# A deformable-convolution, causal-attention and mixture-of-experts kernel: new lengths for the maxima's way and a new written order, the causal mask of the second score pass moved to GpSimd, late weights laid over other room, scatters by pairs of images

## The chip, the cores and the metric

The kernel runs on one core of one Trainium2 chip. The metric is the device time of one execution in microseconds (us). It is the median over the runs that were made. The engines are named as in the profile: PE (TensorE matmul), PEld (its weight load), DVE (VectorE), ACT (ScalarE), POOL (GpSimd) and SP (SyncE, which here only issues DMAs).

## The reference

The input `x` holds 8 images of 56 x 56 positions with 128 channels, so 3136 tokens per image. Layer 0 is a deformable convolution with two residual blocks, layer 1 causal attention followed by a top-8 mixture of 64 experts. Cut to what matters:

```python
# layer 0
xp = x @ w_in + b_in
h = gelu(batchnorm(depthwise_conv3x3(x)))
offset, mask = h @ w_off + b_off, softmax(h @ w_msk + b_msk)      # 4 groups, 9 points
y = einsum("nghwpc,nhwgp->nhwgc", bilinear_sample(xp, offset), mask) @ w_out + b_out
x = x + gamma1 * layer_norm(y)
x = x + gamma2 * layer_norm(gelu(x @ w_fc1 + b_fc1) @ w_fc2 + b_fc2)
# layer 1
t = x.reshape(8, 3136, 128)
z = layer_norm(t)
scores = (z @ Wq) @ (z @ Wk).T / sqrt(3136)
scores = scores + -1e12 * (1.0 - tril(ones))                      # causal
t = t + softmax(scores) @ (z @ Wv)
probs = softmax(layer_norm(t) @ gate_w.T + gate_b, axis=tokens)
vals, idx = top_k(probs, 8)                                       # per image and expert
pooled = sum_k vals * t_normed[idx]
out_e = gelu([pooled, 1] @ weight1[e])  ->  [., 1] @ weight2[e]   # 64 experts, 512 hidden
t = t + scatter_add(idx, vals * out_e)
```

## The kernel before, in words

**Tiling.** An image is cut into seven chunks of 448 tokens (`CH`), and these into four groups `(b, s)` of one or two chunks, so there are 32 groups. Tiles have 128 tokens. Each stage is a generator over groups: `bring` and `prepare` load the input and project it (L496 to L543), `conv`, `plan`, `fetch`, `weigh` and `sums` do the sampled convolution (L552 to L754), `project` the two residual blocks (L819), `norm` the layer norm (L937), `scores`, `maxes`, `keyed`, `exps` and `attend` the attention, `after` its end and the gate (L1095 and after), `share` prepares the experts' shares.

In the sampled convolution `fetch` loads 1.6 MB (`g<-img`, L683) per tile over SP's queue into one of three buffers, DVE multiplies it by the taps (L707), and POOL folds it by a chain of adds (L726, 3.45 us each, then L746 to L754). For image 0 PE does the rest of the folding (L733).

**Attention.** Scores are computed twice. First with queries in the rows: `scores` (L982) writes `sc` tiles to PSUM, for diagonal tiles a second small matmul (L990, `identb` times `maskq`) adds the causal mask, and `maxes` (L1005, L1007) reduces each row to its negated maximum `neg`. Then with keys in the rows: `keyed` (L1047) writes `st`, for which the maximum of each query must be in the contraction itself. So the maxima take a way through memory: `neg` (one value per partition) is written by a DMA on ACT's queue to a row in DRAM (L1013, L1017), and a DMA on SP's queue reads that row into row 0 of `qT` (L1019). The first `st` matmul of the group needs it. Because row 0 of `zT` is 1, `st` comes out with the maximum subtracted. For the 224 pieces that cross the diagonal, a second matmul (L1055, `identb` times `maskk`) adds the mask to `st`; ACT takes the exponential into `pe` (L1068, three buffers), and `attend` multiplies it with the values (L1079). `maskk` is made at the start: GpSimd builds the mask (masks.py:30), PE transposes it (`pt_mask`, L472), ACT copies it (L474).

**What sets the order.** The steps are not ordered by a scheduler at build time. Every `yield need(engine, us, since=...)` marks one step with the engine's length in us and, in `since`, the time from which it can start. A planner, run beforehand, took these numbers and wrote the string `ORDER`, one letter for each step (`NAMES` tells which generator a letter advances). The kernel replays that string, so each engine's queue has exactly this order. The numbers in `need` don't reach the chip; they act only through the string. In `maxes` the planner is told that the read can be issued 4.0 us after the write and that the row is there 2.6 us after that.

**The end.** When all groups are projected, `give_up` (L1365) frees the convolution's room and loads the first 20 experts' weights (`weights`, L1411 and L1413: pairs of experts, 1 MB a pair, on SP's queue). After the last step of `ORDER` the work pool `wk` is closed, and a pool `fin` takes its room: 12 late experts' weights first, then the tiles `outT`, `rows`, `eh`, `hb`, `eo`, `oe`. The tail runs the experts four at a time (`hidden` L1453, `turned`, `outputs` L1482, `gathered`), between which POOL gathers the rows of the output that will be changed (`gather`). The remaining weights follow as experts are done with. At last, for each of four pairs of images, PE and DVE add the experts' outputs to the gathered rows (L1550, L1553); when all four pairs are done, one block of 32 indirect DMAs on POOL writes them back (L1558).

A second kernel in the file, taken for inputs with large offsets, is left out here.

Of the kernel before, what the change touches and what calls it, by code (L numbers as in the profile page):

```python
# [8 lines left out]
F32 = mybir.dt.float32  # L9
BF16 = mybir.dt.bfloat16  # L10
# [3 lines left out]
ALU = mybir.AluOpType  # L14
# [60 lines left out]
def need(engine, us, take=None, give=None, since=None, kind=None, when=None, lock=False):  # L75
# [27 lines left out]
    "ppppppbpbkppppbwpwwwpwpwpvkvfvvvvvvvwvpfpccpccwcpwwcbwccfcppccpcccwpcwpccpcbwcvcvcvcvcvcvccv"  # L103
    "cvvwggvvwsvwwvvvvwsvvvgfsvppcccspbccpgppbpscgcpfsscccspcpccvcfsscsvcvcvvcsmvcvcmvfvcvmcvcmvc"
    "vcvmmcvmcvmmvcvmcmvmmgmgvpbmpvgspcmpkscpvmgcfssmsmmmmmpssnpnnnnsfvncvncngpnnsnnncfspncvqqxqv"
    "qgvpgscccfxsscxxgxsvbvcssxvfccsvcgxcctscteftvstvevaevaeavacsvcvcvavocfpcospmccoompoocpcoppoc"
    "opbcbpmggcommoomosoccmococmmpomcmgcsmgmfmpmvcvcvssvcvcsoccccmfsssvcmgcmoscmgsmommfmvmvmcvsgc"
    "vmvcmskmvcmfsvmvmmgmmmcmscmcvvcvmfssvvovooopcgscpcpfssgmpcmgpppmsmmmkmpcfssnmnpgcmspmcmcfncs"
    "smncncmcnmgcscmnvcmfssnmmcmmgnsmnnvbmnvnfvnnvncgcssngcmncmnscnmvvcnfmssmmnmnmvmvnqmgcscvvkcc"
    "xqfsqxcvqmqxxqcmxqxqxcvqcxqcxbsmxqqmqxxmxqvmcmxqmvsvvvvmxfsvgpqpqcmmxgspmxmgxbmskcmpxgpmvcfs"  # L110
    "xtctectcmmcamcmsstesvcmvescvtsesvtsfcvtmtagaaeeameaevasmatatvestvenvtnsntsnnstnsfnentgvaaeae"
    "naeaevgasnvanvmntvnsnmtesctnsageseasfnatnemnacmnmsavonvmmsvnmcsmvnscvnmpcgnbmcpcvcvcoqcqxoxc"
    "qocqqcxoxcqxomxqksmsoqxfqxoqxoqxqxmoqxqxsmqxqmxcqmxsqxcqmmcqxcmxxqmqxoqxmoqxqosmoqqxoxqxqxqs"
    "xosxoqsfxomoxpmxopmgcmspmpmmosmmcxbgscvmsoscmsfocogxpttsetvtvsevaesaecvscmscvokamvfagomtcoet"
    "coamcmomtomseocseacoavostoposestssptfgetetppottsapnnannsanenpnbesnesttpntpgpabpsasfaepeeagpa"
    "etatespttvcstnvnavssavesnctfesangnteanntensvanvenvansvensvanssensfganqqqcqxcxqxqxqcxqxcxqcxq"
    "xcqxqxcqxgqccacaqqcxxcqxqcxqcxxqxqsgxcxqvcscqcsqxsvxqscxsfqxvqcxqccxqcxqsxvmqxmqxsvmxsqsvmsv"
    "qsfxqxtxtcectecsgtettsamaevaescmasvsagcfetcaetcqecqcvcqxqvxcqcxcxqcxmaxacmqcamcxcqgmmqmpobpx"
    "mxqompxopxmoppbmopomoooooxoompkmxotptemttommetmemtmptvavaevtevomvamvomevoavmavaomteetetootot"
    "ooaaemoaoaemeomemoammotmmoommotmoemooomakmaaemtmtmemtmsentnnmntnmsnannmestmtassaseamfetenmaa"  # L120
    "aetesnateanteannaesannanmgsntnstsesaesfnmtngnmnnstneaseqmqxsqxsqxssfqxqgqmamsamxxstxmmssqmsq"
    "xsfemgsxmqmstxkstemtetxsmtgssfaaeceagcsceavmmmcamsacxvsmctsvmsctvsfmgxcteteaesmavavetmcvaesv"
    "ctvsctsectsecftmctctavcaegcaeaecaevacamcapbmcpomocmmgpcmcmocmmtmcpmopccvcevvmvoktmoaootemote"
    "oteomamaematmsotaeomvtmsvemvvtsmvtstoasmaennnansmnasfnnnemeameaamanmmogcmmnmmsnmnccmsncncsnc"
    "snsvsfvovnmnvgnvnvosnvnvonvsvnksmqssqxfqcxmqxqxsqcxqxcmoqxoqmoxqoxsoqmxoqcxsmocxqvsmqsxsmxfq"
    "mcomxvcomvqqcomxqxqmcqxcmxqcxqxqmcxmcxqmcvmxcomvmxvpmcmvcbomovcmvocpvoxcooomcpkcpcxtgmttemet"
    "etpmmtmmsanaennaennnaesnnaagnottesntesoaesnasgnsfonantntteenaeatosteaoetosonoanososeonoasnos"
    "fonagnntnoqeqgxqxsoqoxqoxqoxsoqxosqxosqosxosfqxqxqxqxgmqsmmsqmqxxqssxsasfxagoqoosqoxqxmxqxqs"
    "mxqxsqsxmsqxsfmoxmogcmmsommoccsmomgsposmotbsosmfccgpsemqmqcqxxqkcmcxaxvsqmmqmsmscqmsqcxsfxcq"
    "xqxtxxtegstteaseaesqcsqcssfqxxtxtgxtetaspeaspaecpsaxcaesapsampsfnonnnnxtpeomapsogppmpstbstes"  # L130
    "bposesgftptegptavnaeavasnvnotontnosvenevtsevstnsvmsnfvtvangaeaecaecaoaocoqocooqxmqxocqmqcxxq"
    "xmcqmqcxqoxqxxqxqcoxocqxoqxoqxocomxsogqmmcqsmmocqxmsxqcoxqxqxsgcsxsfqvcvcqxoxtovtesvovtcosva"
    "evsoeavsoscavcsfcovctgoteteaecsavmccttsomtsecmscsooocfcegccpcqpcqcqxcpcxxcbapaemcqkapcxacmgc"
    "apqbmpttexpmxmaepampmtmvtevmvtmexvmvtmvttexvmavmavaeemaemmammammtmmtmememtkmttemamaemmaemsaa"
    "mstmtestetsesttsasfaeaeaeaamsanonmntsotsentmnenanensmasganftmeosnannotgntmeoetosnoanooemonos"
    "onmoomssagsnasfmnmnnmmnonmtnqqsoxqoxemxssogsososfomotqeoqxosqmxqxqxqmxkqxsomxaosmaxmsgossfto"
    "teocomgoscamoceosavooxmststsecsftcgtxetetvmasoavaecsevtevasccsvasevafcvacvmcvtmctctemgeamate"
    "tectetcvptbgcacetacaecmeamaecaapcmommocpcoptmcmocttomopomocotmomvevvcvecovcomakvmaataemotoma"
    "momomsevomvomvosnmeennonansmoansonaosomtntestmoanfeeanamaonnmnomnnsmmgcnmmnommcnscmngcmncovv"
    "cocvvsvcnovmnovkcnvonvoqscosqcxsqsmfxqxvqxqvxpoxqosqpoxqxqmxvqbxsqxmsqmxsqsxsfqxmqxpxqmmqxsm"  # L140
    "xqmpmpxsopmcsqbqscspqmxfxqcmqcpxcxmcxmxocmocmomcommocpommgoxomcpmcccoxtcvoectoctcevoteotooot"
    "oomoakmooaageoeaeamaootomtmomemstogaeotaesoaeotaetonsanteasonensanosnasnfnovmotvmovemnovovmt"
    "vsteteansaesnagsnasnsfntnteotnoaensoooatntseenstnsgtsensftnganeaneqmqxsmqxqxmsxqmqsxmsxsagms"
    "faaqeqqxsxaqxqxsaqxosxqsosqsfxoxqomxqmgsmqmmsqmsqxgsmxsxsfxgmscmoccsoqvckspsxqbpsmqocfxqxqmx"
    "qxqmqxxqxqmmpmsssxmxqmspsmxpsnfnpmnqnonqxnqpxqxqmxnoqnxmqxoqbxnmxnpoxmnonmgnmmnqmxmosoqmpmpq"
    "xxmtxoxtegttsoaetoesgaoeqsesqvsqsfoqomvgovovoocsxccxxqcxscvqcxqssxqxsqsfxcmtgmtamaetesctxakm"
    "somemaocsmaecosmcaogsmcfamomococmvqcqxocqoqmqxxqcmxqxcxqcxqxcqxtoooctcetxectvecgttsqaaevgqev"
    "axsxqeqxsmxcmssvcmscqsfqxmmxvamvxacsvacvttvetstevecasvaesmvxcsatsvfmmgtvxpmtcmscpccsaecbspsm"
    "spetkcppfgcamcaaemetcaemcmpacmmsampbmmpptsgmttstesteseasvsfaevaevavavtvmtvesvaemvatsmeststse"
    "gsftettamgasetetasaeaessaesasfatatnennaennannsnototnegteoetcnntcntcnocancnagnsenonasesnsansf"  # L150
    "eonoaonoonoomonocqmqcxqcxcqxqoxqxqxqsxoqoxoqxosmxooagsmsmosscfommoxcomcomcvscvgcsvcxvssvtcsv"
    "tsfevtexgtectctsctavaevsmvesakmcsacsfacemtgeaevaapcopmtcmmtcbemmpctpocageoceaocpaovctocvmvtm"
    "cevmcevtmvtcvtectvacvaeomaeaecomoaatomatmeoemoammaommotommoototmoemoeeoomaokatmaaomtotommeme"
    "omseanonmnnomnsntonnmeontmotoaaseaeomaanasmossosnfmnmonnmonnmosnomooonsoommonosgcnsmsnsfmnnm"
    "ccngqcvscmvxovovvmvsqkmqcqsxxqxomqxoqxosmoqsxosfqmoxqoxcqmxqxcmqsxcqmcqxcsxqoqxosxmsxqmscfmx"
    "qcmqcqxmxqxmqxqxoxmovxomvmocmmvcovcmmgmmxmcvpbmcpccgxovoctoctectgcpemetkcmtcvacvaecvtepamopp"
    "abemmpammsanmnnpmnoootsteptsnptntmnsensetsmvsfavaveaevaeatantveaetstentntsntnsngassannmfeaea"
    "smanemnamensagnntnsnestsnsgqesfqaaqxsxqxqqxxsqxqxssqxsqxsfqxqxqxtxsgteteteqsqqssxaxssfmexgcm"
    "mqmmsqcmxgcxsmcscqmsqcsxcsfmxgcccscmqcmcsqqkcvmxaxpsmabmsapqmsmqmsfxmxpmxmancqmqsxqxqxmnqxqx"
    "smpqnqsnpsnqxnqxqxsxnqcfxnmnxcqxnnxpcmxoncgmpcncmmpmconmxcbqcgmmcomxtsteomgessqpgqsxpqsxsvxq"  # L160
    "sfxqxqxqxvoaoacootocootceootceoaexmovakmvagtmtetesaeoqmmosqxomqosxoqsxosmqsofxqoxqoxvqxqxqsv"
    "qxxaxsqvosmqsoxsmxsofmgmoqmoqomqxsqmxqxxmsqxmqsxmsxsamgsfmcmmommcgstcmvotvsxtovtsvsomevssfvv"
    "egemamasaeacmootccxktsevtesvtsevstctfavxaevmtemvmamsagsaettseatesteascmscpsfmctcpmgtmpsaaeps"
    "apcbasecepsabpssafgtepettseptgptstvmavaevsavessvaesfgaemaattcevstevaveavcastctesgctesaecsasf"
    "attemeamatactnenoncenctnncntecnacoaenagamcncnomcmscogmmcscmmsvcscomstcfsvtcvtvmvcvcsvcocecsm"
    "ectkesmctsctsoancofoaeomvntevsanmnvtemagnneanseavaoasoonotntgontenasesnesmcafmnmoqqoxcqxoqoc"
    "xocpxqpcqxqxcopbocoqpcqxopcoxaoxtvgcoectcoaceovqovovtotoeteooottxavxmeavmtvemvtvmtaaemxaemaa"
    "emeamxatameommommoamoomotomotoemoeoomoakmattotmeotemmaotmemseaotnonmnnosmnnmonnsamoanooaotte"
    "moeaesmasassfemnanmnamnnmmsnsmmgcnsmmsnsnsfmnnccvncvcmnvgsvvcovcnvsvmnokvmqvsqoxqcxqmxcqxcoq"
    "xcqxvopxqbsmqmoxpqxsqmofxvqxsmqmqxmcqmcmsxqmxqxsqxxqmxqxsqmxsqsxooqfxqxmxpmxpmcmmcoocommcomm"  # L170
    "oxmocppbmocpoocoxcgotoctectctgecaeaeacacgtcmceokmatmtoetemmoemmstotmamnsnoemnootostmootosnos"
    "anmonaeoaesmnaofnatteaevtnevaovaevasnvnanvmntmntnvetsvnengeansaensoasnosnsfpnonpmnoqosqoxoqx"
# [2207 lines left out]
```

## The time and the profile before

| | |
|---|---|
| median of 3 runs | 3163.42 us (3162.01 to 3168.71) |
| profiled execution, its time | 3155.84 us |
| profiled execution, its span | 3154.0 us, mean granted PE clock 0.952 |
| PE busy in 0 to 143 us, 143 to 2921, 2921 to 3154 | 80.1 of 143, 2597.1 of 2778, 122.5 of 233 |
| DVE busy in the same stretches | 107.7, 2071.6, 84.7 |
| POOL busy in the same stretches | 73.8, 2057.1, 104.9 |
| first start of `sc` (L982), last start of `av` (L1079), weight loads | 121.1 us, 2962.2 us |
| 32 scatters (L1558), first and last issue | 3096.7, 3136.6 us, 0.98 us each |

The profile is of one execution. Its span is the time from the first to the last instruction, and the execution takes 1.8 us more. PE's busy time is high in the middle stretch, where the convolution of later images runs beside the attention of earlier ones. At the start and in the tail no engine is busy throughout. A line of the groups is: line, engine, operation, output and inputs, shapes and count, then busy time and mean of one in ns, then the idle time of the engine just before these instructions with what ended it. A line of the waits is: who waited, for what, us in total, times, the longest.

### The profile page before, as it was taken

How to read it: one execution, taken by the hardware profiler on the slowest of the kernel's cores; microseconds unless marked ns; L12 is line 12 of the kernel's file. 1: busy time of each engine (PE TensorE's matmuls, PEld its weight loads, DVE VectorE, ACT ScalarE, POOL GpSimd, SP SyncE). 2: the span in 40 equal slices, each digit the busy share in tenths (PEclk: the TensorE clock that was granted, in tenths of full speed). 3: DMA queues.
4: the chain of work that ended last, by engine and by line, in shares of the span. 5: the costliest groups of instructions: out<-in, count | busy, mean ns of one | idle time of the engine just before them, and what ended most of it. 6: DMA issues, size and time to landing. Idle time of an engine off the chain costs nothing.

```text
span 3154.0 us, 37084 instructions
## 1 busy us (share of the span) xinstructions
PE 2799.6 (89%) x11986; PEld 1655.0 (52%) x11986; DVE 2264.0 (72%) x4101; ACT 1497.9 (47%) x3489; POOL 2235.8 (71%) x2322
## 2 busy tenths in 40 slices
PE   4789899998998989998998999999998999899771
PEld 3666555555555545555555555555554555555331
DVE  6888893788768786677877788678878865467630
ACT  3444445554555435653555545644464455523310
POOL 3767784787678877688877889678977998123453
PEclk9889999999999999999999999999999999999896
DMA  6665443445353444345534445356642553030170
GB/s 175 212 217 187 149 155 76 130 147 191 118 162 116 145 138 170 95 145 166 181 128 106 167 139 190 95 139 187 184 97 87 197 163 112 23 134 12 63 282 26
DMA packets 300849, 442.45 MB, mean 140 GB/s; under 512 B 39812, under 2 KB 153996, under 8 KB 300644
## 3 DMA queue, kind: packets, MB, share of 16 engines
q1 hardware_dynamic: 184612, 382.32, 36.0%
q10 hardware_dynamic: 112768, 51.50, 7.1%
q0 software_dynamic: 3264, 6.15, 0.7%
q8 instruction: 97, 1.59, 0.2%
q14 instruction: 108, 0.88, 0.1%
HBM read 386.27 MB, written 53.81 MB: 140 GB/s over the span
## 4 chain that ended last, share of the span: by engine, by line
PE 65%; DVE 12%; DMA 11%; POOL 6%; issue 3%; ACT 2%; ACTq 0%; SPq 0%; POOLq 0%; DVEq 0%
PE sc L982 16%; PE st L1047 15%; PE av L1079 14%; DMA maxes<-neg 7%; PE ph L857 4%; PE pm L869 3%; DVE g L707 3%; DMA g<-img 2%; DVE pv L568 2%; POOL g L726 1%; DMA qT<-maxes 1%; DVE mx L1005 1%; PE py L843 1%; PE pg L1151 1%; PE pc L1108 1%
## 5 line engine op out<-in xcount | busy, mean ns | idle before, releaser
L707 DVE TENSOR_TENSOR g<-g,tp 128x3200 f32<-128x3200 f32 (+1 forms) x200 | 694.7, 3477 | 100.8 <-DMA g<-img 78.4
L1047 PE MATMUL st<-qT,zT 128*128 128x448 f32 (+8 forms) x1606 | 664.1, 537 | 114.5 <-DMA qT<-maxes 99.5
L726 POOL TENSOR_TENSOR g<-g 128x1536 f32<-128x1536 f32 (+1 forms) x200 | 690.4, 3452 | 94.1 <-DVE g L707 85.6
L1068 ACT ACTIVATE pe<-st 128x448 f32<-128x448 f32 (+8 forms) x803 | 396.5, 504 | 616.8 <-PE st L1047 327.5
L982 PE MATMUL sc<-zT,qT 128*128 128x512 f32 (+4 forms) x1594 | 620.1, 523 | 12.9 <-DVE mx L1005 12.1
L1079 PE MATMUL av<-pe,zk 128*128 128x448 f32 (+8 forms) x1606 | 617.0, 510 | 3.1 <-ACT pe L1068 2.0
L1005 DVE TENSOR_REDUCE mx<-sc 128x1 f32<-128x512 f32 (+6 forms) x797 | 442.5, 584 | 140.3 <-PE sc L982 97.5
L1047 PEld LDWEIGHTS st<-qT,zT 128*128 128x128 f32 (+1 forms) x1606 | 289.9, 199 | 358.4 <-issue 246.5
L1079 PEld LDWEIGHTS av<-pe,zk 128*128 128x128 f32 (+1 forms) x1606 | 288.3, 192 | 235.1 <-issue 182.2
L982 PEld LDWEIGHTS sc<-zT,qT 128*128 128x128 f32 x1594 | 275.9, 188 | 255.1 <-issue 122.5
L568 DVE SCALAR_TENSOR_TENSOR pv<-xg,dw,pv 128x448 f32<-128x448 f32 x448 | 307.6, 687 | 49.2 <-ACT pv L565 38.1
L746 POOL TENSOR_TENSOR g<-g 128x768 f32<-128x768 f32 (+1 forms) x175 | 317.9, 1817 | 8.9
L857 PE MATMUL ph<-xT,fc 128*128 128x512 f32 (+2 forms) x448 | 214.5, 572 | 23.6 <-DVE xT L795 23.1
L861 ACT ACTIVATE hid<-ph,b_fc 128x512 f32<-128x512 f32 (+2 forms) x224 | 140.7, 634 | 159.9 <-PE ph L857 152.8
L659 POOL TENSOR_TENSOR taps<-taps,a 128x252 f32<-128x252 f32 (+1 forms) x288 | 190.3, 661 | 17.8
L649 POOL TENSOR_TENSOR a<-w 128x756 f32<-128x756 f32 (+1 forms) x96 | 135.9, 1415 | 83.5 <-DVE w L640 76.8
L869 PE MATMUL pm<-fc,hid 128*128 128x128 f32 x1600 | 194.4, 279 | 0.0
L869 PEld LDWEIGHTS pm<-fc,hid 128*128 128x128 f32 x1600 | 183.5, 192 | 11.8 <-issue 11.6
L748 POOL TENSOR_TENSOR g<-g 128x384 f32<-128x384 f32 (+1 forms) x175 | 175.4, 1002 | 11.1
L1285 POOL TENSOR_TENSOR share<-share,part 128x512 f32<-128x512 f32 x56 | 71.0, 1268 | 133.4 <-DVE part L1275 132.7
L778 POOL TENSOR_SCALAR ssb<-ssb 128x4 f32<-128x4 f32 (+1 forms) x56 | 11.2, 199 | 179.1 <-ACT ub L776 161.9
L857 PEld LDWEIGHTS ph<-xT,fc 128*128 128x128 f32 x448 | 78.9, 197 | 82.2 <-issue 32.6
(263 smaller groups left out, 4150.8 us busy)
## 6 DMA issues: line engine op xcount, KB each, us to landing
g<-img SPq DMA_DIRECT2D x192, 1600.0 KB
w1t<-in_L_ffn_weight_dram SPq DMA_DIRECT2D x32, 512.0 KB
w2t<-in_L_ffn_weight_dram SPq DMA_DIRECT2D x32, 512.0 KB
xin<-in_x_dram SPq DMA_DIRECT2D x56, 224.0 KB
xTd<-xc ACTq DMA_DIRECT2D x56, 224.0 KB
img<-st ACTq DMA_DIRECT2D x112, 112.0 KB
out_dram<-t ACTq DMA_DIRECT2D x24, 448.0 KB
od<-o ACTq DMA_DIRECT2D x24, 448.0 KB
```

The source lines that it names most:

```text
L568: nc.vector.scalar_tensor_tensor(p3, src, dw[:, k : k + 1], p3, op0=ALU.mult, op1=ALU.add)
L659: nc.gpsimd.tensor_add(dst, dst, a5[:, :nt, kx])
L707: nc.vector.tensor_mul(g3, g3, tp[:n, lt % 4].unsqueeze(2).to_broadcast([n, NTAP * NG, 32]))
L726: nc.gpsimd.tensor_add(g[:n, : 12 * C], g[:n, : 12 * C], g[:n, 12 * C : 24 * C])
L746: nc.gpsimd.tensor_add(g[:n, : 6 * C], g[:n, : 6 * C], g[:n, 6 * C : 12 * C])
L857: nc.tensor.matmul(ph[:, :n], fc1[:, f * P : (f + 1) * P], xT[:, :n], start=True, stop=True)
L869: nc.tensor.matmul(four(pm, m)[:, i, :], hid[:, f, i * P : (i + 1) * P], fc2[:, f, :], start=False, stop=i == m - 1 and f == 3,)
L982: nc.tensor.matmul(pp[:w, :n], qT[:, i * P : i * P + w], zTs[b, g][:, k0 : k0 + n], start=True, stop=not diagonal,)
L1005: nc.vector.tensor_reduce(mx[:w, i, j : j + 1], pp[:w, :n], AX.X, ALU.max)
L1047: nc.tensor.matmul(pp[:w, :n], zTs[b, g][:, j * P : j * P + w], qT[:, u * CH + q0 : (u + 1) * CH], start=True, stop=m <= 0,)
L1068: nc.scalar.activation(pe[:w, :n], pp[:w, :n], AF.Exp, scale=SCALE)
L1079: nc.tensor.matmul(av[:, q0:CH], zs[b, g][:w, j, :], pe[:w, : CH - q0], start=first, stop=last)
```

## The change

- `maxes`: the planner is told 12.0 us from write to read and 3.5 us from read to use, instead of 4.0 and 2.6. In `project` a DVE step is told as 0.345 us instead of 0.32.
- The mask of the second pass: `maskk`, its transpose and copy, and the 224 matmuls L1055 are gone. After the exponential, GpSimd's `affine_select` puts zeros into the upper triangle of `pe` for the same 224 pieces; `exps` has one more step for each of them.
- `ORDER` is planned anew from these numbers, as a whole.
- The tail's pool `fin`: `rows`, `outT` and two buffers each of `eh`, `hb`, `eo` are laid first, the late weights after them, so they lie at other addresses. Late experts are 14 instead of 12.
- The scatters: one block of eight after each pair of images, instead of one block of 32 after the last pair. Only the last block waits for all.

```diff
 ORDER = (
-    "ppppppbpbkppppbwpwwwpwpwpvkvfvvvvvvvwvpfpccpccwcpwwcbwccfcppccpcccwpcwpccpcbwcvcvcvcvcvcvccv"
...
+    "ppppppbpbkppppbwpwwwpwpwpvfvvvvvvvvfwvpwpwwcwcpwccpwcbpckccfcwwwwccppcpcccpcpccpbcvcvcvccvvcv"
...
-    maskk = cst.tile([P, P], BF16, tag="maskk", name="maskk")
...
-        yield need(PE, 0.2, take="gen")
-        pt = gen("pt_mask")
-        nc.tensor.transpose(pt[:, :P], mask, ident)
-        yield need(ACT, 0.3, give="gen")
-        nc.scalar.copy(maskk, pt[:, :P])
...
-                yield need(DVE, 0.32)
+                yield need(DVE, 0.345)
...
-        at = yield need(SP, 0.1, since=at + 4.0)
+        at = yield need(SP, 0.1, since=at + 12.0)
         nc.sync.dma_start(qT[:1, :N], row[:N].rearrange("(o n) -> o n", o=1))
-        yield need(DVE, 0.0, since=at + 2.6)
+        yield need(DVE, 0.0, since=at + 3.5)
...
-            at = yield need(PE, 0.00168 * n + 0.056 * (m > 0), take="gen", since=since)
+            at = yield need(PE, 0.00168 * n, take="gen", since=since)
...
-                stop=m <= 0,
-            )
-            if m > 0:
-                nc.tensor.matmul(
-                    pp[:w, :m], identb[:w, :w], maskk[:w, m0 : m0 + m], start=False, stop=True
-                )
+                stop=True,
+            )
...
             nc.scalar.activation(pe[:w, :n], pp[:w, :n], AF.Exp, scale=SCALE)
+            if m > 0:
+                at = yield need(POOL, 0.2 + 0.0013 * m)
+                nc.gpsimd.affine_select(
+                    out=pe[:w, :m],
+                    in_=pe[:w, :m],
+                    compare_op=ALU.is_ge,
+                    fill=0.0,
+                    base=m0,
+                    pattern=[[1, m]],
+                    channel_multiplier=-1,
+                )
...
-    ELATE = 12
+    ELATE = 14
...
     fin = ctx.enter_context(tc.tile_pool(name="fin", bufs=1, reuse_waits="tile"))
+    homed = [fin.tile([P, K, C], F32, tag="rows", name=f"rows{p}", bufs=NB // 2) for p in range(NB // 2)]
+    outT = fin.tile([P, NB, E], F32, tag="outT", name="outT")
+    ehs = [fin.tile([P, 512], F32, tag="eh", name=f"eh{j}", bufs=2) for j in range(2)]
+    hb2 = [fin.tile([P, 4, EB, NB], F32, tag="hb", name=f"hb{j}", bufs=2) for j in range(2)]
+    eos = [fin.tile([P, C], F32, tag="eo", name=f"eo{j}", bufs=2) for j in range(2)]
     homes = [(experts["pool"], "w1t", "w2t", EFIRST // EG)] * (EFIRST // EG)
     homes += [(fin, "w1l", "w2l", ELATE // EG)] * (ELATE // EG)
...
-    outT = fin.tile([P, NB, E], F32, tag="outT", name="outT")
...
+    done_ = nc.alloc_semaphore("scattered")
     for p in range(NB // 2):
...
             nc.vector.tensor_add(r[:, k0 : k0 + 4], r[:, k0 : k0 + 4], pf)
-    done_ = nc.alloc_semaphore("scattered")
-    with tc.tile_critical(no_gpsimd_drain=True):
-        for p in range(NB // 2):
+        with tc.tile_critical(no_gpsimd_drain=True):
             for k in range(K):
                 nc.gpsimd.indirect_dma_start(
...
                 ).then_inc(done_, 16)
-        nc.gpsimd.wait_ge(done_, 16 * K * NB // 2)
+            if p == NB // 2 - 1:
+                nc.gpsimd.wait_ge(done_, 16 * K * NB // 2)
```

## The prediction

> **What bounds the kernel now.** I read the page first (busy shares, chain), then PE's waits, then single stalls.
>
> ```profile
> span 3154.0 us, 37084 instructions
> PE 2799.6 (89%) x11986; PEld 1655.0 (52%) x11986; DVE 2264.0 (72%) x4101; ACT 1497.9 (47%) x3489; POOL 2235.8 (71%) x2322
> ...
> PE 65%; DVE 12%; DMA 11%; POOL 6%; issue 3%; ACT 2%; ACTq 0%; SPq 0%; POOLq 0%; DVEq 0%
> PE sc L982 16%; PE st L1047 15%; PE av L1079 14%; DMA maxes<-neg 7%; PE ph L857 4%; PE pm L869 3%; DVE g L707 3%; DMA g<-img 2%; DVE pv L568 2%; POOL g L726 1%; DMA qT<-maxes 1%; DVE mx L1005 1%; PE py L843 1%; PE pg L1151 1%; PE pc L1108 1%
> ```
> PE is the bound, 65% of the chain; the largest foreign share is the maxima's way (`neg` to DRAM, back into row 0 of `qT`): 7% + 1%. In the waits of PE:
>
> ```profile
> PE st L1047 <- DMA qT<-maxes: 99.5, 19, 7.3
> PE ph L857 <- DVE xT L795: 23.1, 14, 6.4
> PE ptg L733 <- POOL g L726: 21.5, 12, 6.9
> ```
> 19 of the 32 groups stop PE here, 99.5 us in all, over four times the next wait. One way in the timeline (image 0's third group), from the write's issue to the read's and to the first `st`:
>
> ```profile
> 356.99 0.38 ACTq L1013 DMA_DIRECT2D maxes<-neg  x1
> ...
> 370.79 0.25 SPq L1019 DMA_DIRECT2D qT<-maxes  x1
> ...
> 373.05 5.07 PE L1047 MATMUL st<-qT,zT 128*128 128x448 f32 x8 [7.27 <-DMA qT<-maxes]
> ```
> 13.8 us for the write, 2.3 more to the first `st`. The windows of the same place (time, PE, PEld, DVE, ACT, POOL busy, PE's clock, DMA):
>
> ```profile
> 356.00:364.00 8.00, 7.80 (x50) 5.86 (x49) 7.70 (x10) 4.49 (x10) 7.68 (x7) 1.00 0.88 230
> 364.00:373.20 9.20, 1.93 (x17) 1.77 (x17) 4.80 (x4) 2.35 (x4) 6.45 (x7) 0.80 0.69 103
> 373.20:376.40 3.20, 3.20 (x5) 1.56 (x6) 2.97 (x5) 0.54 (x1) 0.00 (x0) 0.50 1.04 378
> 376.40:384.40 8.00, 8.00 (x24) 3.08 (x24) 4.68 (x5) 5.26 (x16) 3.02 (x3) 1.00 0.55 198
> ```
> PE idles 7.3 us and then runs 3.2 us at half clock: a stall costs twice.
>
> [...] 1.00 or 0.50, low windows of 3.4 to 10 us behind nearly every such stall. [...] here the write of 3.5 KB in single elements takes 9.1 to 14.6 us mostly, [...]
>
> **1. Way of the maxima.** Where it is the limit, last `sc` to first `st` is 13.3 to 19.5 us, about 15. The planner's lengths go from 4.0 + 2.6 to 12.0 + 3.5, so more PE work is ordered in between. I summed that work (mean duration of each form in the trace) for each group in both built orders. Before, 19 groups have under 15 us (mostly 8 to 10), shortfall 102 us, which meets the 99.5 of the trace. After, seven have: images 0 (11.6, 12.5, 9.7), 3 (7.8), 4 (14.8), 6 (6.4), 7 (9.0): 33 us. The read also moves on SP's queue: it now stands behind 12 `g<-img` fetches and 11 `xT` loads. A load issued behind a fetch lands with it, 6 to 8 us, alone in 2.4, so I add 3 us for the short groups concerned: 40. And in group (7,1) it stands behind 17 of the early experts' weight loads, which before came after it:
>
> ```profile
> 2772.84 0.59 SPq L1411 DMA_DIRECT2D w1t<-in_L_ffn_weight_dram  x1
> ...
> 2792.15 0.67 SPq L1413 DMA_DIRECT2D w2t<-in_L_ffn_weight_dram  x1
> ```
> Twenty loads took 19.3 us to issue, and by the trace's completion events each landed 4.3 us (first) to 10.8 us (from the tenth) after its issue. Ten go ahead of the write's landing, seven must follow it, then the read: 7 x 1.0 + 10.8 = some 18 us after the landing in place of 2.3, so +15 (5 to 25). What is left: 55. Gain 99.5 - 55 = 44 (25 to 100; the upper end if every idle in those intervals, 142 us, shrinks alike).
>
> **2. Clock.** By form, PE's work in half-clock windows behind way stalls took 43 us more than at full clock, 2.3 per stall. Eleven of 19 stalls go: 25 (15 to 40).
>
> **3. Mask matmuls.**
> ```profile
> L1055 PE MATMUL st<-maskk,identb 128*128 128x128 bf16 (+1 forms) x224 | 48.1, 215 | 0.0
> ...
> masks.py:30 POOL TENSOR_SCALAR_AFFINE_SELECT mask<-mask x1: 292/292/292, 53.6 to 53.6; 128x128 f32<-128x128 f32 x1
> ```
> Their 48.1 us overlap their neighbours: start to start, a 448-wide `st` takes 0.808 us with a mask and 0.752 without. 224 x 0.056 = 12.6 off PE, on the path.
>
> **4. Selects.** 224 x 0.292 = 65 us more on POOL (2236 to 2301, 73% of the span), between Exp on ACT and `av` on PE; `pe` has three buffers, so a late select also holds the third next Exp. Cover: PE's work between a diagonal piece's `st` and its `av` is 4.1 us in the median after (4.0 before), needed are 0.5 (Exp) + 0.3 and the handovers, if POOL is free. 23 selects stand directly behind an `L726` add of 3.45 us, 18 behind one of 1.8. At 0 to 1 us each for these, little for the rest, I take 8 (0 to 25). Queued behind a waiting select are the `g` adds that L733's transposes wait for (21.5 us now); Exp mostly runs ahead, so nothing more is added.
>
> **5. Start.** PE's transpose `pt_mask` waited 7.2 us for the mask. It goes; DVE is busy 108 of the first 143 us and is late next. 3 (0 to 7).
>
> **6. Table loads.** The order raises ACT's table loads from 164 to 180: 16 x 1.283 = 20.5 us on an engine busy 47%. Cover is that idle half: 0; if each hit a chain, -20, kept in the range.
>
> **7. Late weights.** Their first pairs are issued at 2962.7, 2978.9 and 2992.3; laid higher they need not wait for the last `av` and gate tiles and come some 19 us sooner. But no PE wait names a weight load; the tail waits for DVE, POOL and the expert chain, whose order is unchanged. Gain 0. Streaming now overlaps the gathers of `gx` (2.6 us) and `rows` (5.6): -2 (-6 to 0).
>
> **8. Scatters.** Each of 32 takes 1.29 us of POOL, in a block whose first issue was at 3096.7, 2.1 us after the last add. Pair 0's adds end at 3085.3, so its first scatter can start 9.3 us sooner. Each pair's matmuls and adds (3.1 us) hide in eight scatters (10.3). Three more block entries at up to 2 us: -5. Gain 4 (-2 to 8). The costs of 0.345 in `project` and 14 late experts add no instruction.
>
> **Sum.** 44 + 25 + 12.6 - 8 + 3 + 0 - 2 + 4 = 79. The profiled execution is 3155.8 (span 3154.0), so 3077; the runs' median lies 7.6 higher, at 3163.4: 3163.4 - 79 = 3084.
>
> **Rivals.**
> (a) Smaller gain: other chains turn late when the fill work is moved (`ph` behind `xT`, `ptg` behind POOL, both already on the waits list), or the way grows to 18 us because fetches now run beside the write: shortfall after 58, plus the weight stall at 25 and selects at 25. 3163 - (99.5 - 83 + 18 + 12.6 - 25 + 4) = about 3137. For it: POOL and DVE are over 70% busy. Against: for the other dependent pairs of PE's pieces the missing cover sums to 60 us before and 63 after.
> (b) Larger gain: all idle of those intervals goes (142 to 40), clock 40, no weight stall, selects free: 102 + 40 + 12.6 = 155, so 3009. Against: seven groups remain short by count.
> (c) Slower: [...] Each select waits behind adds, and PE's `av` behind it. Without selects the gain is 87, so it decides from 87 / 224 = 0.39 us of PE wait per select; at 0.6 it is 134 and the time 3163 - 87 + 134 = 3210. Against: 96 selects follow another select, and cover is 4 us.
> (d) It doesn't do what it says: the lengths are planner numbers, the two DMAs are unchanged. If fill is nominal and SP's order delays the reads, way and clock give nothing: 3163 - 12.6 + 8 - 3 - 2 = about 3154.
>
> **Chances.** Forecast (3060 to 3110) 0.52; (a) 0.19; (b) 0.18; (c) 0.05; (d) 0.06, of which 0.02 within 0.2%. A measurement here can tell some 0.2%, 6 us, from no change. Range 3030 to 3130, which takes in most of (a) and of (b). Faster 0.93, same 0.02, slower 0.05.
>
> **What would show it.** After: PE's waits with `st <- qT` at 40 to 60 us in 7 to 10 times, the longest (over 12 us) in group (7,1) near the weights' issue; mean clock up from 0.952; no L1055; POOL + 65 us; `av <- POOL pe` under 15 us; scatters from some 10 us before the last add. Wrong if `av <- POOL` tops 40 us, if `ph` or `ptg` waits double, or if no long stall stands at (7,1).

## The result, and the profile after

The kernel after takes 3135.89 us (median of 4 runs, 3131.22 to 3141.48), the kernel before beside it on the same chip 3165.89. The ratio is 0.9905, with a 95% interval of 0.9885 to 0.9924: 30 us faster (24 to 36), where 79 had been forecast. Among the rivals it lies at (a), 3137.

The page of the kernel after: span, busy times, and the shares of the chain that ended last.

```profile
span 3129.5 us, 36846 instructions
PE 2783.2 (89%) x11761; PEld 1646.7 (53%) x11761; DVE 2265.1 (72%) x4101; ACT 1515.5 (48%) x3504; POOL 2295.3 (73%) x2546
...
PE 63%; DVE 11%; POOL 11%; DMA 8%; issue 3%; ACT 2%; POOLq 0%; another core or an unknown queue 0%; ACTq 0%; SPq 0%; DVEq 0%
```
DMA's share of the chain fell from 11% to 8%, POOL's rose from 6% to 11%. The way left the chain and something else came in. The mean granted clock is 0.947 (0.952 before): it did not rise.

PE's waits in the kernel after (who waited for what: us in total, times, longest):

```profile
PE st L1043 <- DMA qT<-maxes: 37.6, 5, 25.8
PE ptg L729 <- POOL g L722: 33.6, 10, 16.5
PE ph L853 <- DVE xT L791: 17.1, 9, 6.1
PE sc L978 <- DVE mx L1001: 14.3, 8, 3.1
...
PE av L1083 <- DVE avs L1092: 9.8, 2, 5.3
...
PE ptp L1240 <- DVE t L896: 8.3, 1, 8.3
...
PE po L589 <- DVE om L597: 6.7, 3, 2.4
...
PE st L1043 <- ACT xg L519: 5.9, 1, 5.9
```
The first line was 99.5 us in 19 waits; it is 37.6 in 5, and 25.8 of them are one wait. The last four lines were not among the 22 longest kinds of wait before. In each of them the instruction waited for made no input of the waiting matmul: `om` is no input of `po`, `avs` none of `av`. It read a PSUM buffer that the matmul is about to overwrite.

The one long wait stands where it was forecast, in group (7,1). The timeline of the kernel after: the write of the maxima on ACT's queue, the weight loads and the read on SP's, and then PE. The single line with a colon is from the waits of SP's queue (who waited for what: us, times, longest):

```profile
2713.83 0.37 ACTq L1009 DMA_DIRECT2D maxes<-neg  x1
```
```profile
2715.79 0.47 SPq L1417 DMA_DIRECT2D w2t<-in_L_ffn_weight_dram  x1
2731.05 0.37 SPq L1415 DMA_DIRECT2D w1t<-in_L_ffn_weight_dram  x1
...
2736.81 0.67 SPq L1417 DMA_DIRECT2D w2t<-in_L_ffn_weight_dram  x1
2738.20 0.25 SPq L1015 DMA_DIRECT2D qT<-maxes  x1
```
```profile
SPq L1415 <- DMA maxes<-neg: 14.8, 1, 14.8
```
```profile
2720.80 0.22 PE L986 MATMUL sc<-maskq,identb 128*128 128x128 bf16 x1
2746.83 2.58 PE L1043 MATMUL st<-qT,zT 128*128 128x448 f32 x3 [25.81 <-DMA qT<-maxes]
```
SP's queue itself stood still for 15 us between two weight loads. By the trace's completion events the eleventh load waited there for the write of the maxima to land, at 2731.03. It shares no data with the write; it waits for the semaphore that the write counts up (number 103 in the trace), and then uses this semaphore itself. So ten of the twenty loads went ahead of the read only after the write had landed. The read was issued last, and its row landed at 2746.70, 15.7 us after the write. The write itself took 17.2 us from issue to landing beside these loads. In e4 below, where the loads come later, it takes 9.3, and in the kernel before, where they do too, the same group's takes 10.1.

The windows of both kernels, cut at the first `sc` and the last `av` (columns as in the prediction: time, length, busy PE, PEld, DVE, ACT, POOL, PE's clock, DMA's share, GB/s). Before:

```profile
0.00:121.00 121.00, 66.11 (x404) 56.95 (x404) 87.82 (x158) 42.08 (x95) 60.62 (x113) 0.96 0.61 191
121.00:2963.00 2842.00, 2652.60 (x10763) 1555.52 (x10763) 2117.84 (x3772) 1436.17 (x3351) 2085.01 (x2119) 0.97 0.44 138
2963.00:3154.00 191.00, 80.89 (x819) 42.52 (x819) 58.30 (x173) 19.64 (x44) 90.13 (x91) 0.73 0.41 148
```
After:

```profile
0.00:124.00 124.00, 67.98 (x403) 58.52 (x403) 90.03 (x159) 45.05 (x100) 62.29 (x115) 0.84 0.59 188
124.00:2935.00 2811.00, 2629.59 (x10539) 1545.23 (x10539) 2120.35 (x3778) 1450.71 (x3361) 2144.09 (x2341) 0.97 0.45 139
2935.00:3129.50 194.50, 85.67 (x819) 42.91 (x819) 54.76 (x166) 19.71 (x44) 88.94 (x90) 0.73 0.40 143
```
The middle is 31.0 us shorter: PE is busy 23.0 less and idle 8.0 less (189.4 to 181.4). The start is 3.0 longer, the tail 3.5. That is the whole 24.5 between the two spans. The way's waits fell by 62 us, yet PE's idle time by 8, so 54 us of other idle came in. Where?

To see it I sorted every idle interval of PE in the middle by what released it: the maxima's row (way); an instruction whose output the waiting matmul reads (data); or one whose output it does not read, so that only the PSUM buffer it freed can be meant (buffer).

| kernel | way | data | buffer | sum |
|---|---|---|---|---|
| before | 99.5 | 53.0 | 37.1 | 189.6 |
| after | 37.6 | 50.2 | 93.7 | 181.5 |

(The sorting repeats: e8 below, the kernel before with another end on another chip, gives 97.1, 54.4 and 36.6. The kernel after repeats less well: e3 below, with another layout alone, gives 32.7, 46.9 and 85.2.) Data waits are what they were. The waits for PSUM buffers are 57 us longer. The kernel has a ring of five such buffers (`ps`, L266), and three more with names of their own. Most of the growth is the ring's, from 32 to 80 us; `av`, a single buffer, goes from 1 to 10. One interval of 2.3 us is sorted as a buffer's although the instruction named for it (`bmvd`, L911) reads no PSUM.

### The profile page after: what moved, and what is told of

Same layout as the page of the kernel before. It is cut to its first block, busy times and chain, and to the rows that moved or that the text cites. A ratio compares the mean times of both kernels' runs of the same rounds, so it can differ in the third digit from the quotient of the medians.

```text
span 3129.5 us, 36846 instructions
## 1 busy us (share of the span) xinstructions
PE 2783.2 (89%) x11761; PEld 1646.7 (53%) x11761; DVE 2265.1 (72%) x4101; ACT 1515.5 (48%) x3504; POOL 2295.3 (73%) x2546
## 3 DMA queue, kind: packets, MB, share of 16 engines
q1 hardware_dynamic: 184612, 382.32, 37.6%
## 4 chain that ended last, share of the span: by engine, by line
PE 63%; DVE 11%; POOL 11%; DMA 8%; issue 3%; ACT 2%; POOLq 0%; another core or an unknown queue 0%; ACTq 0%; SPq 0%; DVEq 0%
PE st L1043 14%; PE av L1083 14%; PE sc L978 14%; PE ph L853 4%; PE pm L865 4%; DVE g L703 4%; DMA g<-img 4%; POOL g L722 3%; DMA xTd<-xc 1%; POOL g L742 1%; DVE mx L1001 1%; PE py L839 1%; PE ptg L729 1%; PE pg L1155 1%; DVE pv L564 1%
## 5 line engine op out<-in xcount | busy, mean ns | idle before, releaser
L703 DVE TENSOR_TENSOR g<-g,tp 128x3200 f32<-128x3200 f32 (+1 forms) x200 | 695.2, 3477 | 99.5 <-DMA g<-img 85.9
L722 POOL TENSOR_TENSOR g<-g 128x1536 f32<-128x1536 f32 (+1 forms) x200 | 689.8, 3449 | 60.1 <-DVE g L703 49.4
L1043 PE MATMUL st<-qT,zT 128*128 128x448 f32 (+8 forms) x1606 | 628.9, 517 | 53.8 <-DMA qT<-maxes 37.6
L978 PE MATMUL sc<-zT,qT 128*128 128x512 f32 (+4 forms) x1594 | 634.5, 528 | 19.3 <-DVE mx L1001 14.3
L1083 PE MATMUL av<-pe,zk 128*128 128x448 f32 (+8 forms) x1606 | 625.4, 510 | 15.6 <-DVE avs L1092 9.8
L742 POOL TENSOR_TENSOR g<-g 128x768 f32<-128x768 f32 (+1 forms) x175 | 318.0, 1817 | 8.1
L1064 POOL TENSOR_SCALAR_AFFINE_SELECT pe<-pe 128x128 f32<-128x128 f32 (+1 forms) x224 | 61.5, 281 | 140.7 <-ACT pe L1060 139.4
L645 POOL TENSOR_TENSOR a<-w 128x756 f32<-128x756 f32 (+1 forms) x96 | 135.9, 1415 | 32.7 <-DVE w L636 26.5
L1092 DVE COPY avs<-av 128x448 f32<-128x448 f32 x56 | 34.7, 620 | 136.5 <-PE av L1083 136.4
```

Of the source, the lines that this page charges most:

```text
L703: nc.vector.tensor_mul(g3, g3, tp[:n, lt % 4].unsqueeze(2).to_broadcast([n, NTAP * NG, 32]))
L722: nc.gpsimd.tensor_add(g[:n, : 12 * C], g[:n, : 12 * C], g[:n, 12 * C : 24 * C])
L742: nc.gpsimd.tensor_add(g[:n, : 6 * C], g[:n, : 6 * C], g[:n, 6 * C : 12 * C])
L978: nc.tensor.matmul(pp[:w, :n], qT[:, i * P : i * P + w], zTs[b, g][:, k0 : k0 + n], start=True, stop=not diagonal,)
L1043: nc.tensor.matmul(pp[:w, :n], zTs[b, g][:, j * P : j * P + w], qT[:, u * CH + q0 : (u + 1) * CH], start=True, stop=True,)
L1083: nc.tensor.matmul(av[:, q0:CH], zs[b, g][:w, j, :], pe[:w, : CH - q0], start=first, stop=last)
```

## The experiments

Three questions: what the way was really worth, what the other parts cost, and why the rest of the idle time grew. The first theory was that the way's stalls had been partly caught up by other engines, so that removing them was never worth their length. The rival: they were worth it, but the new order, which puts more fill work under the way, takes that work from other waits. Letters in the expectations stand for theories as they are named there. Chips differ: the kernel before had medians from 3125.9 to 3165.9 us on those used. So each ratio is to runs of the kernel before on the same chip, and differences between kernels of different chips are taken from the ratios, times 3165.9.

**The way alone (e1, e2).** The same edit in the kernel before and in the kernel after:

```diff
+    asides = [indram(f"aside{j}", [GT * P]) for j in range(2)]
...
-        nc.sync.dma_start(qT[:1, :N], row[:N].rearrange("(o n) -> o n", o=1))
+        nc.sync.dma_start(asides[(NGRP * b + s) % 2][:N].rearrange("(o n) -> o n", o=1), row[:N].rearrange("(o n) -> o n", o=1))
```


> The kernel before, where the maxima are read back into a row of DRAM instead of row 0 of qT: both DMAs still run, but st waits for nothing of them, and the maximum is not subtracted (row 0 keeps what the copy left there). Theory A (catch-up: while PE stood in these waits, DVE, ACT and POOL worked off what was late, so the stalls also paid for other delays): far less than the stalls' worth is gained, 30 to 70 us, and PE's other waits, most of them for DVE, grow by 40 us or more. Rival B (the stalls were worth their full length, and the new written order put other waits in their place): the 99.5 us of waits and some 40 us of half clock behind them go, 110 to 140 us, and the other waits stay as they were.

> The same edit in the changed kernel (maximum not subtracted). There 37.6 us of way waits are left, 25.8 of them in group (7,1). Theory A: 25 to 40 us faster than the changed kernel, since most of it is the one stall near the end, where little of the convolution is left to catch up with; it ends above 3090 us. Rival B: the same here, but since in the order of before everything is gained by the same edit, the two no-way kernels then lie with the before one below the after one.

Measured: e1 0.9688 [0.9668, 0.9708], 3038.75 against 3140.47, so 102 us less than before. e2 0.9865 [0.9839, 0.9891], 3095.84. The middle's idle is 98.5 in e1 (data 59.4, buffer 38.6) and 143.4 in e2 (data 50.0, buffer 93.4). PE's waits in e1:

```profile
PE ph L858 <- DVE xT L796: 21.5, 14, 5.4
PE ptg L734 <- POOL g L727: 20.7, 10, 6.6
PE ptp L1237 <- DVE po L1232: 20.6, 4, 6.6
```
and in e2:

```profile
PE ptg L730 <- POOL g L723: 35.8, 12, 17.0
...
PE av L1084 <- DVE avs L1093: 9.8, 2, 5.3
...
PE ptp L1241 <- DVE t L897: 8.3, 1, 8.3
...
PE po L590 <- DVE om L598: 7.1, 3, 2.8
```
So catching up falls for the old order: with the way's waits gone from it, hardly anything took their place (data and buffer 98 us against 90), and the time fell by 102 us, no less than the 99.5 of the waits, though below rival B's 110 to 140. In the new order e2 is only 13 us faster than the kernel after by the ratios, where both theories had put 25 to 40, although 37.6 us of way waits went. Without the way the new kernel is 57 us slower than the old one, and the buffer waits of the kernel after stand there unchanged. They belong to the new kernel's order and its selects, not to the way.

**The layout of the late weights undone (e3).** `fin` as before: late weights first, `ELATE = 12`, one buffer each.

> The changed kernel with the late weights laid as before (12 late experts first in the pool, then the tiles), all else as changed. In the trace of the changed kernel the tail from the last av to the first transpose of outT takes 12 us more than before, with expert matmuls behind loads of weights. Theory: the new layout costs this, so 8 to 12 us faster than the changed kernel. Rival: the tail's loss comes from where SP's queue stood, not from the layout: within 3 us of the changed kernel.

Measured: 0.9902 [0.9884, 0.9921], against 0.9905 for the kernel after. The layout is worth nothing that can be told; my expectation of a loss from it missed.

**The read ahead of the weights (e4).** The 20 early weight loads are issued only after the read of group (7,1), the thirtieth of the 32 groups (`READS` is 29):

```diff
-        for e in range(0, EFIRST, EG):
-            weights(e, ep, "w1t", "w2t", EFIRST // EG)
+        pending.append(ep)
...
+            if pending and lines["maxes"].at > READS:
+                ep = pending.pop()
+                for e in range(0, EFIRST, EG):
+                    weights(e, ep, "w1t", "w2t", EFIRST // EG)
```


> The changed kernel, the 20 early weight loads issued only after the read of group (7,1) has been issued. Theory: the 25.8 us wait of (7,1) falls to 6 us, and the half clock behind it goes: 18 to 24 us faster. Rival (catch-up also here: DVE or POOL is late in this stretch, or the weights come too late for the first experts): under 8 us.

Measured: 0.9861 [0.9842, 0.9879], 14 us under the kernel after by the ratios, less than the 18 to 24 expected. The wait in e4:

```profile
PE st L1043 <- DMA qT<-maxes: 7.9, 3, 5.2
```
The stall at (7,1) is the weights' doing, and its 25.8 us cost some 14. So in the new order, here as in e2, about half of a removed way wait or less comes back as time.

**More fill in the old order (e5).** If the way only needs more PE work under it, the old order with the second pass's steps of 17 groups moved later should do as well. Only letters of `ORDER` change places:

```diff
...
-    "qgvpgscccfxsscxxgxsvbvcssxvfccsvcgxcctscteftvstvevaevaeavacsvcvcvavocfpcospmccoompoocpcoppoc"
+    "qgvpgscccfxsscxxgxsvbvcssxvfccsvcgxccscfvsvvvvcsvcvcvvcfpcspmccmpcpcppcpbcbpttetteaeaeaaaooo"
...
```


> The kernel before with its own written order, in which only the first keyed, exps and attend steps of 17 groups stand later: steps of other lines were taken from just behind them and put ahead, so that more PE work lies in the maxima's way (summed with the mean durations: shortfall below 15 us 102 before, 34 here, 33 in the changed kernel). No other part of the change. Theory B (the stalls are worth their full length, and what the changed kernel lost is in the rest of its new order): 68 us of waits and some 25 us of half clock go, 75 to 95 us faster than before, so faster than the changed kernel by 45 us or more. Rival A (cover taken from elsewhere opens the same waits there, whoever plans it): 30 us or less.

Measured: 1.0957 [1.0929, 1.0985], 3471.34 against 3165.22. PE's waits in e5:

```profile
PE st L1047 <- ACT pe L1068: 81.7, 12, 23.3
PE av L1079 <- ACT pe L1068: 67.8, 10, 31.3
PE pq L530 <- ACT xg L515: 47.7, 8, 19.4
...
PE st L1047 <- DMA qT<-maxes: 25.0, 7, 6.6
```
The way's waits fell further than in the kernel after, to 25.0, and the time rose by 306 us, which neither theory had. Moved crudely, the second pass comes in lumps, and ScalarE's exponentials become the wait. Cover for the way is not free; this shows how dear it can be, not what a careful order pays.

**The selects: old order, and left out (e6, e7).** e6 is before with the selects in place of the mask matmuls. e7 is after without the `affine_select`:

```diff
             nc.scalar.activation(pe[:w, :n], pp[:w, :n], AF.Exp, scale=SCALE)
+            if m > 0:
+                nc.gpsimd.affine_select(out=pe[:w, :m], in_=pe[:w, :m], ...)
```


> The kernel before with GpSimd's selection in place of the 224 mask matmuls, each select right behind its exponential's step in the order of before; nothing else changed. Theory: 12.6 us of PE go, the start gains 3, the selects cost 5 to 10: 5 to 12 us faster. Rival C (65 us more on POOL, in a queue that folds the samples, are what the changed kernel lost): 20 us or more slower.

> The changed kernel without the 224 selects, so that the second pass has no causal mask at all. Theory B: only the select's own cost on PE comes back, 3 to 10 us faster than the changed kernel. Rival C (POOL's load makes DVE and PE wait): 25 us or more faster.

Measured: e6 1.0149 [1.0128, 1.017], 47 us slower than before; e7 0.9855 [0.9829, 0.9881], by the ratios 16 us faster than after, between the two ranges. PE's waits in e6:

```profile
PE st L1043 <- DMA qT<-maxes: 92.8, 18, 8.9
PE av L1081 <- POOL pe L1062: 50.7, 44, 6.2
PE ptg L729 <- POOL g L722: 29.3, 12, 14.6
```
In the old order 44 selects arrive late, for 50.7 us. This fits rival (c), which had them wait behind the `g` adds, but what stood ahead of these 44 is not shown. One such wait in the trace of the kernel after: the exponential of a 64x64 piece ends at 162.63 us, and its select starts at 165.81, as the add ahead of it ends (L722, 162.40 to 165.85). In the new order, which knows of the selects, that wait is 3.8 us in 4 times, yet leaving the selects out saves 16: the middle's buffer waits fall from 93.7 to 80.3. That fits a late select holding the buffers behind it, through `pe` and the exponentials; that chain is argued, not followed instruction by instruction.

**Masks back on PE (e11).** After, with L1055's matmuls and `maskk` put back and the selects taken out.

```diff
-                stop=True,
+                stop=m <= 0,
+            if m > 0:
+                nc.tensor.matmul(pp[:w, :m], identb[:w, :w], maskk[:w, m0 : m0 + m], start=False, stop=True)
```


> The changed kernel with the mask added by the 224 matmuls again in place of the selects, in the order of the changed kernel. From the run without either (16 us faster than the changed kernel by the ratios) and 12.6 us for the matmuls: 0 to 6 us faster than the changed kernel, so that the swap of mask for select gave nothing. Rival (the matmuls lie beside other work, or the selects' cost is elsewhere): 10 us or more in either way.

Measured: 0.9915 [0.99, 0.993]; the kernel after's 0.9905 lies inside. Mask matmul and select cost the same here, and the swap is worth nothing that can be told.

**Scatters by pairs alone (e8).** Before, with the end of the kernel after.

> The kernel before with the scatters by pairs of images alone. In the changed kernel's trace the first scatter starts 2.1 us after the first pair's adds and the 32 follow each 1.29 us with no pause at the blocks: 9 us faster (8 to 10) if that is all, against 4 in the prediction, which put 5 on the block entries.

Measured: 0.9970 [0.9959, 0.998], 9.3 us less by the medians. The first scatters in the trace of the kernel after (the next ones follow every 1.29 us to the last, across the blocks):

```profile
3071.88 1.03 POOL L1566 DMA_INDIRECT out_dram<-rows,once  x1 [48.31 <-PE pf L1560]
3073.21 1.00 POOL L1566 DMA_INDIRECT out_dram<-rows,once  x1 [0.30 <-issue]
```

**Is VectorE too busy? (e9, e10).** Most of the new buffer waits, 46 us of the 57, end with a VectorE instruction, so VectorE might simply be full. Half of the tap columns are left out, in both kernels, which takes 330 us of work off it:

```diff
-            g3 = g[:n, :].rearrange("p (k c) -> p k c", c=32)
+            g3 = g[:n, :].rearrange("p (k c) -> p k c", c=32)[:, :50]
...
```


> The kernel before, DVE multiplying only 50 of the 100 tap columns (the samples come out wrong): 200 DVE instructions of 3.48 us become about 1.8, some 340 us off DVE's queue, all orders as they were. PE's waits followed back: 53 us of them were DVE's running instructions before, 83 in the changed kernel. Theory D (the new order's cover was bought by putting PE closer behind DVE's queue): here 30 to 70 us faster than before.

> The same edit in the changed kernel. Theory D: 70 to 120 us faster than the changed kernel, so that the difference to the same edit in the kernel before grows from 30 us to 55 to 85, near the forecast. Rival O (the new waits come from steps placed right behind their producers, busy or not): it falls by as much as before does, and the difference stays at 20 to 40 us.

Measured: e9 0.9886 [0.9865, 0.9906], e10 0.9796 [0.9776, 0.9815]. Both fall alike, and the change is worth 31 us between them (3090.64 to 3059.68), as before. The theory of a full VectorE falls. Buffer waits are 30.6 in e9 and 71.6 in e10, a surplus of 41; data waits are 36 in both.

**The best of the parts (e12).** After with e4's and e11's edits together.

> The changed kernel with both repairs: the early weights behind the read of group (7,1), and the mask by matmuls. If the two add up: 14 us from the first and 0 to 6 from the second, 14 to 20 us faster than the changed kernel, the fastest version that leaves nothing out.

Measured: 0.9855 [0.9837, 0.9873], 3081.16 against 3126.74. It ties with e4; these two are the fastest versions that leave nothing out, some 1.4% under before and 0.5% under after. The middle's buffer waits are 78 us here and 93 in e4, which differs from it by the selects: with e7, this puts some 15 of the 57 us down to the selects, not to the order.

**Too few PSUM buffers? (e13 to e18).** If the lack of a sixth buffer is the cause, a sixth must give the kernel after much more than the kernel before. To make room for it, `tp` goes in all six: VectorE reads the taps from SBUF. The sixth buffer (the first lines of the excerpt) is in e14, e16, e17 and e18 only.

```diff
-        return ps.tile([P, 512], F32, tag="ps", name=name, bufs=5)
+        return ps.tile([P, 512], F32, tag="ps", name=name, bufs=6)
...
-                nc.scalar.copy(tp[:, :m]..., taps[:, lt : lt + m]...)
...
-                g3, g3, tp[:n, lt % 4].unsqueeze(2).to_broadcast([n, NTAP * NG, 32])
+                g3, g3, taps[:n, lt].rearrange("p r q -> p (r q)").unsqueeze(2).to_broadcast([n, NTAP * NG, 32])
```


> Control. The tap weights are no longer copied by ScalarE into the PSUM tile tp; VectorE multiplies by them from SBUF. Five buffers ps remain, a PSUM bank stands unused; the shares at the end use a ps buffer and a ScalarE copy, and 18 early experts in place of 20. Both theories: close to the kernel before (within 20 us either way; the multiply may be slower from SBUF), PE's waits for PSUM buffers near the 37 us of before.

> As e13, with six buffers ps in place of five. Theory P (the new order costs PSUM buffers): before's 37 us of buffer waits fall to some 20, so 10 to 20 us under e13. Theory Q (buffer waits only show where an engine is late; the next wait would take their place): 0 to 10 under e13.

> Control: the same edit as e13 in the kernel after. Both theories: the difference to e13 stays at some 30 us (0.99 of it), buffer waits near 96 us.

> As e15, with six buffers ps. Theory P: the 96 us of buffer waits at least halve and the time falls by 35 to 60 us against e15, clearly more than e14 against e13, so that the change with six buffers is worth 50 us or more. Theory Q: e16 falls by no more than e14 does (0 to 15 us), other waits (for data from VectorE and ScalarE) grow in place of the buffers'.

Measured: e13 1.1256 [1.1229, 1.1283], e14 1.1223 [1.1198, 1.1248], e15 1.1444 [1.1419, 1.1469], e16 1.1409 [1.1378, 1.1441]. The controls themselves missed by far: e13 is 396 us slower than before, and with this edit the change makes the kernel 59 us slower (e15 against e13). The groups of GpSimd in the kernel before, and then in e13:

```profile
L726 POOL TENSOR_TENSOR g<-g 128x1536 f32<-128x1536 f32 (+1 forms) x200 | 690.4, 3452 | 94.1 <-DVE g L707 85.6 <-PE po L593 6.6 <-PE pq L530 1.0
L746 POOL TENSOR_TENSOR g<-g 128x768 f32<-128x768 f32 (+1 forms) x175 | 317.9, 1817 | 8.9
```
```profile
L721 POOL TENSOR_TENSOR g<-g 128x1536 f32<-128x1536 f32 (+1 forms) x200 | 729.5, 3648 | 61.8 <-DVE g L702 47.1 <-issue 7.0 <-PE sc L977 4.2
L741 POOL TENSOR_TENSOR g<-g 128x768 f32<-128x768 f32 (+1 forms) x175 | 416.3, 2379 | 8.8
```
GpSimd's adds stretch, the 768-wide one from 1817 to 2379 ns, and its busy time goes from 2236 to 2814 us. In that kernel a sixth buffer is worth 10 us in both orders. Buffer waits in the middle fall by 44 us in the old order and 54 in the new one, and data waits grow by 30 and 52 in their place, as theory Q had it. But GpSimd is 578 us busier there, so the test says little of our kernels. The last two runs make the slower multiply short: six buffers, and only 25 of 100 tap columns.

> As e14 (six buffers ps, tap weights read from SBUF), but only 25 of the 100 tap columns are multiplied, so the sampled sums are not the reference's. With some 1.1 us in place of 4.1 per multiply, [...]GpSimd's busy time should come back from 2814 us to 2240 to 2400. Theories P and Q: some 0 to 60 us under the kernel before, PE's buffer waits under 37 us.

> The same edit in the kernel after; 75 of 100 tap columns are left out. The change was worth 29 to 30 us with five buffers both with all taps and with half of them. Theory P (too few buffers ps cost the new order 59 us): with six it is worth 50 us or more, and after's buffer waits fall from some 75 to 96 us to under 45. Theory Q (the buffer waits only show where an engine is late, and other waits take their place): it is worth 20 to 40 us again.

Measured: e17 0.9987 [0.9975, 0.9999], 3121.04; e18 0.9880 [0.9864, 0.9897], 3088.84. With six buffers the change is worth 32 us; with five it was 30, and 31 with half of the taps. The middle's idle by kind:

| kernel | way | data | buffer | data and buffer |
|---|---|---|---|---|
| before | 99.5 | 53.0 | 37.1 | 90 |
| after | 37.6 | 50.2 | 93.7 | 144 |
| e17 | 83.0 | 48.9 | 31.9 | 81 |
| e18 | 33.0 | 64.4 | 62.7 | 127 |

The order's surplus in buffer waits is 31 us in place of 57. Not all of this fall is the sixth buffer's: with five buffers and half of the taps the surplus was 41 already. The surplus in data waits, which was -3 (0 with half of the taps), is now 16, so the sum of both moves little: 54, 41 with half of the taps, and 46 here. One of PE's waits in e18 holds most of the 16:

```profile
PE av L1078 <- POOL pe L1059: 21.8, 21, 3.8
```
`av` waits 21.8 us for selects, which was 3.8 in the kernel after; in e17 it waits 10.1 for exponentials. That the buffers are only where the new order's lateness shows first, and that with one more of them part of it shows at the data, fits this and the time, but is not shown: GpSimd is still busier in this pair (2355 and 2418 us) than with five buffers (2236 and 2295), and the 21.8 may come from that. What the runs do show is that theory P's 50 us did not come.

## Why the prediction was wrong, step by step

**The step that failed** is the sum's silent assumption that PE's other waits stay, and the sentence that kept rival (a) at 0.19: "for the other dependent pairs of PE's pieces the missing cover sums to 60 us before and 63 after". As a count of data it was near (measured: 53.0 and 50.2). But a matmul also depends on the reader that must empty its PSUM buffer, and these pairs were not in the count. They went from 37.1 to 93.7 us. Of what the way gave, 62 us, the middle's other waits took back 54. e1 and e2 show that this is the price of the new kernel's order: without any way the old kernel wins by 57 us, and no other part of the change costs that (e3 and e11 find nothing, e8 a gain). In time: of the 102 us that the way cost in the old order, 13 are left in the new one (e2), and 57 are paid elsewhere; 102 - 13 - 57 = 32, and 30 were measured. Rival (a) had the mechanism, other chains late because fill work was moved, but named `ph` and `ptg`: `ptg` grew by 12 us, `ph` fell by 6. That its 3137 agrees with the result is luck: it put the gain of the way at 16.5 us, which was 62, and named no buffer waits.

**1, the way.** Direction and place right. Left were 37.6 us in 5 waits against 55 in 7 to 10 forecast, a gain of 62 against 44. The row of (7,1) was forecast at some 18 us after the write's landing, behind seven loads, and came 15.7 after it, behind ten: this term was sized well. What it did not have is that the write, beside the loads, takes 17.2 us and holds the loads themselves back.

**2, the clock.** 25 us forecast. PE's busy time in the middle fell by 23.0; less the masks' 12.6 that leaves 10. The stall in the prediction's windows cost twice (7.3 us idle and then 3.2 us at half clock), but so did new ones: in the kernel after, for example, `av` waits 5.3 us for `avs` until 2266.3, and 5.8 us of PE's work follow at half clock (2265.3 to 2272.1). PE's work inside half-clock windows of the middle was 134.4 us before, 119.4 after and 54.3 in e1, where PE's busy time fell by 42. The old order without the way got the clock's gain, the new order did not. (The forecast's reading of the windows, 3.4 to 10 us, leaves out one of 13.7 us at 2421.)

**3 and 4, mask and select.** 12.6 against 8 forecast. e7 prices the selects at 16, and e11 finds no difference between the two ways. The sum of 4.6 came to nothing. The cover of 4.1 us between `st` and `av` was read rightly (`av <- POOL pe` 3.8 us); what the forecast left out shows, again, in waits for buffers (e7, e12).

**5, the start.** 3 us of gain forecast; the first `sc` comes 3.0 us later. The mask's wait went, but nothing of it is seen in the old order either: in e6, which has no mask transpose, the first `sc` comes at 120.5, and in e5 and e8 on the same chip, which have it, at 120.1 and 121.8. In e7, on that chip too, the new order has it at 124.8, so the delay goes with the new order. The start's clock, 0.96 before and 0.84 after, says nothing of the change: in runs of the old order it is 0.84 (e1) to 0.96 (e5).

**6 and 7.** Table loads: no run isolates them. The layout: forecast at nothing to -2, measured at nothing (e3).

**8, the scatters.** 4 us forecast, 9.3 measured (e8), as much as the 9.3 by which the first could start sooner. The forecast charged up to 2 us for each further block; in the trace of the kernel after scatters follow each other every 1.29 us across blocks, and in e8 there is one pause of 2.2 us, before the last block.

**The other rivals.** (c) forecast what e6 shows in the old order, 47 us slower with 50.7 us of waits for selects. The new order, which was planned with the selects, escapes most of it. (d) falls: the way's waits did go. (b) would have needed the fill work to be free.

**The tail.** It is 3.5 us longer in the profiled execution of the kernel after than in that of the kernel before, but this is no cost of the change. From the start of the last `av` to the end of the span the old end takes 203.9 us in e1 and 203.1 and 203.8 in e5 and e6; the new end takes 192.1 to 197.7 on the same chips (e2, e3 and e4 beside e1; e7 and e8 beside e5 and e6). The 191.7 of the kernel before is, with 191.8 in e9, low among the runs with its end.

**What stays open.** Why this order leaves less slack at so many places: no other planned order was run, so the lengths told to the planner, the selects' steps and chance in its search aren't told apart. How much of the 57 us a sixth buffer would take without the slower multiply and adds of e13 is open too.

## What to carry to other kernels

Work that is put under a long wait can be taken from under other waits: count the cover of every dependence of the waiting engine, the readers that free its buffers as well as the producers of its inputs, before crediting the gain. Take the wait away in both orders to price the wait and the order apart. And when waits for buffers show, add a buffer in both kernels before calling the lack of it the cause.

## What the runs showed of the hardware that was not expected

- With one operand of VectorE's 128x3200 multiply in SBUF instead of PSUM (e13) the multiply took 4144 ns instead of 3477, and GpSimd was busy 578 us longer (2814 instead of 2236), although none of its own instructions was changed; the kernel took 12.6% longer. The mean of the selects on GpSimd went from 281 ns (after) to 501 (e15). With a quarter of the columns (e17) the multiply still takes 1559 ns, and GpSimd is 119 us busier than in the kernel before (2355 us).
- A read of 3.5 KB issued behind ten weight loads of 512 KB on one queue landed 15.7 us after its data was there. The write of that data, 3.5 KB in single elements on another queue, took 17.2 us beside the first ten loads and 9.3 (e4) and 10.1 (before) without them.
- The issuing of those loads stood still for 15 us (14.8 in the waits of SP) until this write had landed, with which they share a semaphore and no data. The line `SPq L1415 <- DMA maxes<-neg` names a transfer that the program does not connect with the waiting one.
- Chips differ by more than the change is worth: 40 us between the medians of the kernel before, against 30.
